# Column maxima of a two-layer graph attention: spread over partitions by a DRAM row instead of by transposes, and scores one step further ahead

## The chip, the core and the metric

The kernel runs on one core of a Trainium2 chip. A core has five engines with a queue each: TensorE (PE in the profile; its weight loads are PEld) multiplies matrices into PSUM, VectorE (DVE) and ScalarE (ACT) work elementwise on SBUF and PSUM, GpSimd (POOL) works on SBUF, and SyncE (SP) issues transfers. ScalarE and GpSimd can issue transfers too. An engine works through its instructions in the order of the program; between engines, semaphores hold an instruction until what it needs is there. The transfers themselves run on 16 DMA engines that the queues share.

The metric is the device time of one execution in microseconds.

## What is computed

There are N = 3327 nodes with D = 512 features. Two layers of attention run first (L = 2, slope 0.01 in the leaky ReLU), with the same dense adjacency mask of zeros and ones:

```
for W in W_stack:                       # two layers
    Wh, Ws = split(x @ W, 2)
    a   = softmax(Wh @ Ws.T, axis=-1) * adj
    x   = leaky_relu(a @ Wh + x)
x = layernorm(x0 + x)                   # x0: the input
xw  = max(sign(x), 0) @ sign(weight).T
out = layernorm(x + relu(adj @ xw))
```

All of the attention is in float32. The softmax needs, for each row of the scores (a query), the row's maximum before the exponential and the sum after it.

## The kernel before

**Tiles.** 3327 rows are NT = 26 tiles of 128, the last with 127 rows. Two tiles make a half chunk (NQ = 13 of them, 256 rows), two half chunks make a chunk (NC = 7, up to 512 rows; the seventh has one half only). Scores are held transposed: keys are on the partitions, queries along the free dimension. A score tile `s` belongs to a half chunk g of queries and a block q of 256 keys: 128 partitions x 2 x 256 float32. The maximum of a query therefore runs over the partitions and over 13 score tiles.

**Stages of a layer.** `project` computes the left and right factors of the scores and the values and stores them to DRAM. `attention` then has one long loop over steps v, with u = v + LOOK. In step v it emits, for the pair (g, q) number v, the aggregation products `values` (L726). For the score pairs, numbered by chunk c, block q and s = 0 or 1, it emits `scores` number u. LOOK = 2 NQ + 4 = 30, so scores run 30 steps ahead; their tiles wait in a ring of SBUFS = 33 SBUF buffers. A layer has 182 score steps and 169 aggregation steps. Hence it begins with steps that have scores alone, goes on with steps that have both, and ends with steps that have aggregation alone.

**Order of the work.** The schedule is written by hand. Each piece of work of a step has a fraction, and the pieces are emitted in order of the fraction (`for _, do in sorted(work, ...)`); every engine keeps that order. A list `after` holds pieces that the next step is to run. For aggregation number v, the step v - 3 emits `shift` (L645, VectorE, fraction 0.0: subtract the query's maximum, the tile `off`) and `exponential` (L648, ScalarE, 0.12). The step v - 2 emits `running` (L656, the sum) and `masked` (L661, the product with the adjacency, then four sums on GpSimd, L699 to L702).

**Scores.** Two score steps make seven products of a Strassen-like scheme (L500). They go to three PSUM banks, X, Y and Z. Between the products to Z, ScalarE copies the bank out (`copied`, L517), and the next product to Z waits for that copy. The order is z1, x2, z6, y5 for s = 0 and z7, y3, z4 for s = 1. VectorE adds up the four quarters and takes the running maximum over the key blocks into `top` (L570). With one half chunk, four plain products and two ScalarE copies (L557) do the same.

**Maxima.** After the last score pair of a chunk (q = 12, s = 1), the three stages of `column_max` are put on `after`:

- `fold` (-0.04): VectorE takes the larger of the two halves of `top` (L594);
- `across` (0.36): TensorE transposes `top` into one PSUM bank (L602, four transposes for a full chunk), VectorE reduces along the free dimension (L605), which leaves each query's maximum in a column of `mx` with queries on the partitions; four multiplications with `ones` (L607) then repeat each column along 128 elements;
- `back` (0.9): TensorE transposes the repeated columns (L612), which puts the maximum of each query on all partitions, and VectorE copies them to `off` (L616), one tile for each half chunk.

For chunk c the last score pair is number 26c + 25. So `across` and `back` stand in step v = 26c - 4, and the first `shift` that reads the new `off` in step 26c - 3. For chunk 0 these steps lie in the part of a layer with scores alone; for chunk 6 they come where the scores have just ended.

**Queues.** SyncE issues all loads of the loop, each some steps ahead: `ws` (two steps), the adjacency (four), `xs` (two) and `gs` (four). GpSimd issues the stores. ScalarE issues no transfer.

Of the kernel before, what the change touches and what calls it, by code (L numbers as in the profile page):

```python
# [9 lines left out]
F32 = mybir.dt.float32  # L10
# [5 lines left out]
ALU = mybir.AluOpType  # L16
# [3 lines left out]
P = 128  # L20
CT = 4
CW = CT * P
HW = CW // 2
# [6 lines left out]
def kernel(  # L30
# [8 lines left out]
    nc = tc.nc  # L39
    N, D = x.shape  # L40
    L = w_stack.shape[0]
# [3 lines left out]
    NC = -(-NT // CT)  # L45
    NQ = NT // 2
# [8 lines left out]
    def halves_of(c):  # L55
        return [g for g in (2 * c, 2 * c + 1) if g < NQ]
# [9 lines left out]
    keep = ctx.enter_context(tc.tile_pool(name="keep", bufs=1))  # L66
# [4 lines left out]
    ps_acc = ctx.enter_context(tc.tile_pool(name="ps_acc", bufs=4, space=PSUM))  # L71
    ps_tr = ctx.enter_context(tc.tile_pool(name="ps_tr", bufs=1, space=PSUM))

    LOOK = 2 * NQ + 4
    SBUFS = LOOK + 3

    def slot(shape, dtype, name):
        return ring.tile(shape, dtype, tag="s", bufs=SBUFS, name=name)
# [2 lines left out]
    make_identity(nc, ident)  # L81
    ident_h = keep.tile([P, P], BF16, name="ident_h")
    nc.vector.tensor_copy(ident_h, ident)
    ones = keep.tile([P, P], F32, name="ones")
    nc.vector.memset(ones, 1.0)
    eps = keep.tile([P, 1], F32, name="eps")
    nc.vector.memset(eps, EPS)
    mv = keep.tile([P, NT, 2], F32, name="mv")
# [17 lines left out]

    xs_d = [tc.dram_tile([NQ, P, 8, 2, P], F32, name=f"xs_d{l}") for l in range(L)]
    ws_d = [tc.dram_tile([NQ, P, 4, HD], F32, name=f"ws_d{l}") for l in range(L)]
    gs_d = [tc.dram_tile([NC, P, 7, 2, HW], F32, name=f"gs_d{l}") for l in range(L)]

    def load_rows(eng, dst, src, r):
# [357 lines left out]
    def attention(l, att):  # L469
# [35 lines left out]
        def scores(c, q, s):  # L505


            mine = halves_of(c)
            if s == 0:
                for i in mine:  # L510
                    sc[i, q] = slot([P, 2, HW], F32, f"s_{l}_{i}_{q}")
            lo, hi = sc[mine[0], q], sc[mine[-1], q]
            c11, c21, c12, c22 = lo[:, 0], lo[:, 1], hi[:, 0], hi[:, 1]

            def copied(name, bank):
                ch[name] = att.tile([P, HW], F32, tag=name, bufs=1, name=f"{name}_{l}_{c}_{q}")
                nc.scalar.copy(ch[name], ch[bank])  # L517

            def z1():
                product(c, q, "Z", A11, B11, True)  # L520
                copied("p1", "Z")

            def x2():
                product(c, q, "X", A12, B21, True)

            def add11():
                nc.vector.tensor_tensor(c11, ch["X"], ch["p1"], ALU.add)

            def z6():
                product(c, q, "Z", S2, T2, False)  # L530
                copied("u2", "Z")

            def y5():
                product(c, q, "Y", S1, T1, True)
                copied("p5", "Y")

            def z7():
                product(c, q, "Z", S3, T3, False)
                copied("u3", "Z")

            def add22():
                nc.vector.tensor_tensor(c22, ch["p5"], ch["u3"], ALU.add)  # L542

            def y3():
                product(c, q, "Y", S4, B22, False)

            def add12():
                nc.vector.tensor_tensor(c12, ch["Y"], ch["u2"], ALU.add)

            def z4():  # L550
                product(c, q, "Z", A22, T4, False)
                nc.scalar.copy(c21, ch["Z"])

            def direct(a, k):
                product(c, q, "D", (A11, A12, A21, A22)[2 * a + k], (B11, B21)[k], k == 0)
                if k:
                    nc.scalar.copy(lo[:, a], ch["D"])  # L557

            def maximum(i):
                t = sc[i, q]  # L560
                if q == NQ - 1 and pad:
                    nc.vector.tensor_scalar(
                        t[:, 1], t[:, 1], there[:, 0:1], there[:, 1:2], ALU.mult, ALU.add
                    )
                if q == 0:
                    top[i] = att.tile([P, 2, HW], F32, tag=f"top{i % 2}", bufs=1,
                                      name=f"top_{l}_{i}")
                    nc.vector.tensor_copy(top[i], t)
                else:
                    nc.vector.tensor_tensor(top[i], top[i], t, ALU.max)  # L570

            if s == 1:

                after.append((-0.05, lambda: maximum(mine[0])))
                if q == NQ - 1:
                    after.extend(column_max(c))
            if len(mine) == 1:
                return [(0.2, lambda: direct(s, 0)), (0.6, lambda: direct(s, 1))]
            if s == 0:
                return [(0.06, z1), (0.31, x2), (0.45, add11), (0.56, z6), (0.81, y5)]  # L580
            return [
                (0.02, z7), (0.2, add22), (0.35, y3), (0.5, add12), (0.68, z4),
                (0.62, lambda: maximum(mine[-1])),
            ]

        def column_max(c):

            n = len(tiles_of(c))
            mx = small.tile([P, CT], F32, tag="mx", name=f"mx_{l}_{c}")
            rep = [top[g][:, 1, ts(a, P)] for g in halves_of(c) for a in range(2)]  # L590

            def fold():
                for g in halves_of(c):
                    nc.vector.tensor_tensor(  # L594
                        top[g][:, 0], top[g][:, 0], top[g][:, 1], ALU.max
                    )

            def across():
                pt = ps_tr.tile([P, CT, P], F32, tag="tr", name=f"ptop_{l}_{c}")
                for i, g in enumerate(halves_of(c)):  # L600
                    for a in range(2):
                        nc.tensor.transpose(  # L602
                            pt[:, 2 * i + a, :], top[g][:, 0, ts(a, P)], ident
                        )
                nc.vector.reduce_max(mx[:, :n], pt[:, :n, :], axis=AX.X)  # L605
                for a in range(n):
                    nc.vector.tensor_scalar(rep[a], ones, mx[:, a : a + 1], None, ALU.mult)  # L607

            def back():
                pb = ps_tr.tile([P, CW], F32, tag="tr", name=f"poff_{l}_{c}")  # L610
                for a in range(n):
                    nc.tensor.transpose(pb[:, ts(a, P)], rep[a], ident)  # L612
                for i, g in enumerate(halves_of(c)):
                    off[g] = att.tile([P, 1, HW], F32, tag=f"off{i}", bufs=1,
                                      name=f"off_{l}_{g}")
                    nc.vector.tensor_copy(off[g][:, 0], pb[:, ts(i, HW)])  # L616

            return [(-0.04, fold), (0.36, across), (0.9, back)]

        def load_adj(g, q):  # L620
            i0, n = half_cols(g)
# [255 lines left out]
        blocks.update(  # L877
            {room[n * len(room) // len(late)]: steps[i] for n, i in enumerate(late)}
        )
        later, after = [], []  # L880
        for v in range(-LOOK - 4, len(steps)):
            u = v + LOOK

            if 0 <= v + WS - 1 < len(steps):
                load_ws(*steps[v + WS - 1])
            if 0 <= v + 4 < len(steps):
                load_adj(*steps[v + 4])
                if blocks.get(v + 4, steps[v + 4]) != steps[v + 4]:
                    load_adj(*blocks[v + 4])
            for lead, load in ((2, load_xs), (4, load_gs)):  # L890
                if 0 <= u + lead < len(ahead):
                    c, q, h = ahead[u + lead]
                    if h == 0 and (lead == 2 or q == 0):
                        load(c, q)
            work, after = after, []
            if 0 <= v + 3 < len(steps):
                s3 = steps[v + 3]
                work += [(0.0, lambda: shift(*s3)), (0.12, lambda: exponential(*s3))]
            if 0 <= v + 2 < len(steps):
                s2 = steps[v + 2]  # L900
                work += [(0.01, lambda: running(*s2)), (0.4, lambda: masked(*s2))]
                of = blocks.get(v + 2)
                if of:
                    work += [
                        (0.6, lambda: halved_sums(*of)), (0.62, lambda: exact(*of)),
                        (0.61, lambda: halved(*of)),
                    ]
                    after.append((0.5, lambda of=of: keep_blocks(*of)))
            if later:
                work += [(0.7, later.pop(0))]  # L910
            if 0 <= u < len(ahead):
                work += scores(*ahead[u])
            if v >= 0:
                work += values(*steps[v])
            if not last:
                work += early.get(v, [])
            for _, do in sorted(work, key=lambda e: e[0]):
                do()
            if v >= 0 and steps[v][1] == NQ - 1:
                later += finish(steps[v][0])  # L920
            if last:
                load_products(v)
# [266 lines left out]
```

## Time and profile before

| What | Value |
|---|---|
| Median of 3 runs | 2652.95 us (2652.05 to 2653.69) |
| The profiled execution, its own time | 2652.55 us |
| Span of the profiled execution | 2650.7 us |
| Mean granted TensorE clock | 0.998 |
| TensorE busy | 2614.6 us, 99% |
| VectorE busy | 2046.3 us, 77% |
| ScalarE busy | 812.1 us, 31% |
| GpSimd busy | 1091.3 us, 41% |
| Moved by DMA | 638.63 MB, 241 GB/s in the mean |

How to read the lines that follow. L726 is line 726 of the kernel. Busy times are in us, the mean of one instruction is in ns. A group has the line, the engine, the operation, what it writes and reads by the program's names, the shape, the count, then busy time and mean, and last the idle time of the engine just before these instructions with what ended it. A line of the timeline begins with the start and the duration in us; a bracket at its end holds the idle time before it and the releaser. A matmul's end is modelled and overlaps the next one, so the cost of one in TensorE's stream is the distance between starts. A line of the windows has the window, its length, each engine's busy time with the number of instructions, the granted clock, the DMA engines' share and GB/s.

### The profile page before, as it was taken

Reading aid. Unit: us, or ns where it says so; the run is one execution under the profiler, and the core shown is the slowest. Engines: PE = TensorE matmul, PEld = TensorE weight load, DVE = VectorE, ACT = ScalarE, POOL = GpSimd, SP = SyncE. Lnnn points to the kernel's source line nnn. Section 1 sums busy time; section 2 is a strip of 40 time slices with the busy share of each in tenths; the row PEclk is TensorE's granted clock in tenths of the full one; section 3 lists DMA queues with packets and bytes.
Section 4 is the critical chain, followed back from the end, with each engine's and each line's share of the span. In section 5 each row is a group of like instructions: output and inputs, shape, how many; then the busy total and the mean of one; then the engine's idle time right before and its main releaser. Section 6 shows DMA issues by size and latency. Waiting matters only on the chain. (4 is left out here: it accounts for less than half of the span.)

```text
span 2650.7 us, 40451 instructions
## 1 busy us (share of the span) xinstructions
PE 2614.6 (99%) x12839; PEld 2271.0 (86%) x12864; DVE 2046.3 (77%) x4211; ACT 812.1 (31%) x2000; POOL 1091.3 (41%) x2029
## 2 busy tenths in 40 slices
PE   9999999999999999999999999999999999999998
PEld 7888888888888888887888888888888888888787
DVE  5554888899888896666754589988899888767976
ACT  3333332333333332221333333333333333222143
POOL 2550343444444444546552044444444444455510
PEclk9999999999999999999999999999999999999999
DMA  5754777777777776776865677777777777677875
GB/s 205 272 193 157 260 239 251 253 266 252 259 244 244 267 248 222 235 245 230 294 219 180 210 231 272 241 257 260 233 270 247 252 255 236 228 260 260 278 245 168
DMA packets 285186, 638.63 MB, mean 241 GB/s; under 512 B 32141, under 2 KB 146671, under 8 KB 283430
## 3 DMA queue, kind: packets, MB, share of 16 engines
q1 hardware_dynamic: 249206, 529.52, 60.4%
q0 software_dynamic: 35760, 106.45, 10.8%
q8 instruction: 105, 1.72, 0.3%
q14 instruction: 115, 0.94, 0.1%
HBM read 528.91 MB, written 106.93 MB: 240 GB/s over the span
## 5 line engine op out<-in xcount | busy, mean ns | idle before, releaser
L500 PE MATMUL pZ<-gs,xs 128*128 128x256 f32 x2496 | 636.2, 379 | 1.7 <-ACT u L517 1.7
L699 POOL TENSOR_TENSOR as<-s 128x128 f32<-128x128 f32 x338 | 163.4, 484 | 1037.0 <-DVE s L661 691.9
L500 PEld LDWEIGHTS pZ<-gs,xs 128*128 128x128 f32 x2496 | 473.3, 190 | 67.8 <-ACT u L517 3.6
L726 PE MATMUL acc<-ws,s 128*128 128x256 f32 x1352 | 402.6, 379 | 0.0
L726 PE MATMUL acc<-wh,s 128*128 128x256 f32 x1352 | 355.9, 379 | 0.0
L726 PE MATMUL acc<-ws,as 128*128 128x256 f32 x1352 | 349.7, 380 | 1.8 <-POOL as L701 1.2
L648 ACT ACTIVATE s<-s 128x512 f32<-128x512 f32 x338 | 213.3, 631 | 377.7 <-DVE s L645 377.1
L500 PE MATMUL pY<-gs,xs 128*128 128x256 f32 x1248 | 320.7, 379 | 2.2 <-ACT p L517 2.2
L726 PEld LDWEIGHTS acc<-ws,as 128*128 128x128 f32 x1352 | 255.2, 190 | 42.3 <-issue 5.8
L726 PEld LDWEIGHTS acc<-wh,s 128*128 128x128 f32 x1352 | 257.3, 190 | 35.2
L726 PEld LDWEIGHTS acc<-ws,s 128*128 128x128 f32 x1352 | 256.2, 190 | 34.4
L570 DVE TENSOR_TENSOR top<-top,s 128x512 f32<-128x512 f32 x312 | 225.4, 735 | 69.0 <-ACT s L557 48.5
L500 PEld LDWEIGHTS pY<-gs,xs 128*128 128x128 f32 x1248 | 236.7, 190 | 36.0 <-ACT p L517 3.8
L645 DVE TENSOR_TENSOR s<-s,off 128x512 f32<-128x512 f32 x338 | 249.2, 737 | 0.1
L661 DVE TENSOR_TENSOR s<-s,adj 128x512 f32<-128x512 f32 x338 | 236.8, 701 | 9.4 <-DMA adj<-in_adjT_dram 1.0
L656 DVE TENSOR_TENSOR total<-total,s 128x512 f32<-128x512 f32 x312 | 231.8, 743 | 0.0
L517 ACT COPY u<-pZ 128x256 f32<-128x256 f32 x312 | 115.8, 371 | 345.5 <-PE pZ L500 344.9
L701 POOL TENSOR_TENSOR as<-s 128x128 f32<-128x128 f32 x338 | 204.7, 606 | 26.5
L726 PE MATMUL acc<-wh,as 128*128 128x256 f32 x676 | 203.0, 382 | 0.0
L700 POOL TENSOR_TENSOR s<-s 128x128 f32<-128x128 f32 x338 | 183.3, 542 | 27.6
L702 POOL TENSOR_TENSOR as<-s,as 128x128 f32<-128x128 f32 x338 | 180.7, 535 | 26.5
L542 DVE TENSOR_TENSOR s<-p,u 128x256 f32<-128x256 f32 x156 | 66.8, 428 | 151.7 <-ACT u L517 151.7
(206 smaller groups left out, 3883.9 us busy)
## 6 DMA issues: line engine op xcount, KB each, us to landing
ws<-ws_d SPq DMA_DIRECT2D x338, 512.0 KB, 3.8
xs<-xs_d SPq DMA_DIRECT2D x182, 512.0 KB, 5.8
adj<-in_adjT_dram SPq DMA_DIRECT2D x324, 256.0 KB, 4.2
xs<-xs_d SPq DMA_DIRECT2D x156, 384.0 KB, 6.5
gs_d<-gsp POOLq DMA_DIRECT2D x88, 256.0 KB, 2.8
gs<-gs_d SPq DMA_DIRECT2D x12, 1792.0 KB, 10.9
adj_d<-ab POOLq DMA_DIRECT2D x169, 112.0 KB, 3.8
ahl<-adj_d SPq DMA_DIRECT2D x78, 224.0 KB, 4.7
```

What stands on the lines that cost most here:

```text
L500: nc.tensor.matmul(ch[bank], xs[c, q, a][:, k], gs[c][:, b, k], start=(start and k == 0), stop=(k == 1), skip_group_check=True,)
L517: nc.scalar.copy(ch[name], ch[bank])
L570: nc.vector.tensor_tensor(top[i], top[i], t, ALU.max)
L645: nc.vector.tensor_tensor(s, s, off[g].to_broadcast([P, 2, HW]), ALU.subtract)
L648: nc.scalar.activation(sc[g, q], sc[g, q], AF.Exp)
L656: nc.vector.tensor_tensor(total[g], total[g], sc[g, q], ALU.add)
L661: nc.vector.tensor_tensor(s, s, adj[g, q], ALU.mult)
L699: nc.gpsimd.tensor_tensor(s3, a11, a21, ALU.subtract)
L700: nc.gpsimd.tensor_tensor(a21, a21, a22, ALU.add)
L701: nc.gpsimd.tensor_tensor(s2, a21, a11, ALU.subtract)
L702: nc.gpsimd.tensor_tensor(s4, a12, s2, ALU.subtract)
L726: nc.tensor.matmul(acc[g][i // 2][:, i % 2], a[i], b[i], start=(q == 0 and i % 2 == 0), stop=(q == NQ - 1), skip_group_check=True,)
```

## The change

The `back` stage no longer uses TensorE and VectorE. `across` ends with a DMA, issued by ScalarE, that stores `mx` to a row of 512 floats in DRAM (`off_d`, one row for each chunk and layer). `back` consists of one DMA for each half chunk, issued by ScalarE too, which reads 256 floats of that row onto each of the 128 partitions of `off`. The four multiplications with `ones`, the second four transposes and the copies out of PSUM are gone, and with them the tile `ones`.

`back` moves one step later than `across` (list `after_next`) and to the fraction 0.15. LOOK becomes 31: for chunk c, `across` now stands in step v = 26c - 5, `back` in 26c - 4, and the first `shift` that reads `off` still in 26c - 3. The ring of score tiles stays at 33 buffers, as SBUFS is now LOOK + 2.

```diff
@@ -71,8 +71,8 @@
     ps_acc = ctx.enter_context(tc.tile_pool(name="ps_acc", bufs=4, space=PSUM))
     ps_tr = ctx.enter_context(tc.tile_pool(name="ps_tr", bufs=1, space=PSUM))
 
-    LOOK = 2 * NQ + 4
-    SBUFS = LOOK + 3
+    LOOK = 2 * NQ + 5
+    SBUFS = LOOK + 2
 
     def slot(shape, dtype, name):
         return ring.tile(shape, dtype, tag="s", bufs=SBUFS, name=name)
@@ -81,8 +81,6 @@
     make_identity(nc, ident)
     ident_h = keep.tile([P, P], BF16, name="ident_h")
     nc.vector.tensor_copy(ident_h, ident)
-    ones = keep.tile([P, P], F32, name="ones")
-    nc.vector.memset(ones, 1.0)
     eps = keep.tile([P, 1], F32, name="eps")
     nc.vector.memset(eps, EPS)
     mv = keep.tile([P, NT, 2], F32, name="mv")
@@ -106,6 +104,7 @@
 
     xs_d = [tc.dram_tile([NQ, P, 8, 2, P], F32, name=f"xs_d{l}") for l in range(L)]
     ws_d = [tc.dram_tile([NQ, P, 4, HD], F32, name=f"ws_d{l}") for l in range(L)]
+    off_d = [tc.dram_tile([NC, CW], F32, name=f"off_d{l}") for l in range(L)]
     gs_d = [tc.dram_tile([NC, P, 7, 2, HW], F32, name=f"gs_d{l}") for l in range(L)]
 
     def load_rows(eng, dst, src, r):
@@ -573,7 +572,8 @@
 
                 after.append((-0.05, lambda: maximum(mine[0])))
                 if q == NQ - 1:
-                    after.extend(column_max(c))
+                    for part, stages in zip((after, after_next), column_max(c)):
+                        part.extend(stages)
             if len(mine) == 1:
                 return [(0.2, lambda: direct(s, 0)), (0.6, lambda: direct(s, 1))]
             if s == 0:
@@ -587,7 +587,6 @@
 
             n = len(tiles_of(c))
             mx = small.tile([P, CT], F32, tag="mx", name=f"mx_{l}_{c}")
-            rep = [top[g][:, 1, ts(a, P)] for g in halves_of(c) for a in range(2)]
 
             def fold():
                 for g in halves_of(c):
@@ -603,19 +602,19 @@
                             pt[:, 2 * i + a, :], top[g][:, 0, ts(a, P)], ident
                         )
                 nc.vector.reduce_max(mx[:, :n], pt[:, :n, :], axis=AX.X)
-                for a in range(n):
-                    nc.vector.tensor_scalar(rep[a], ones, mx[:, a : a + 1], None, ALU.mult)
+                nc.scalar.dma_start(
+                    out=off_d[l][c].rearrange("(a p) -> p a", p=P)[:, :n], in_=mx[:, :n]
+                )
 
             def back():
-                pb = ps_tr.tile([P, CW], F32, tag="tr", name=f"poff_{l}_{c}")
-                for a in range(n):
-                    nc.tensor.transpose(pb[:, ts(a, P)], rep[a], ident)
                 for i, g in enumerate(halves_of(c)):
                     off[g] = att.tile([P, 1, HW], F32, tag=f"off{i}", bufs=1,
                                       name=f"off_{l}_{g}")
-                    nc.vector.tensor_copy(off[g][:, 0], pb[:, ts(i, HW)])
-
-            return [(-0.04, fold), (0.36, across), (0.9, back)]
+                    nc.scalar.dma_start(
+                        out=off[g][:, 0], in_=off_d[l][c][ts(i, HW)].partition_broadcast(P)
+                    )
+
+            return [(-0.04, fold), (0.36, across)], [(0.15, back)]
 
         def load_adj(g, q):
             i0, n = half_cols(g)
@@ -877,7 +876,7 @@
         blocks.update(
             {room[n * len(room) // len(late)]: steps[i] for n, i in enumerate(late)}
         )
-        later, after = [], []
+        later, after, after_next = [], [], []
         for v in range(-LOOK - 4, len(steps)):
             u = v + LOOK
 
@@ -892,7 +891,7 @@
                     c, q, h = ahead[u + lead]
                     if h == 0 and (lead == 2 or q == 0):
                         load(c, q)
-            work, after = after, []
+            work, after, after_next = after, after_next, []
             if 0 <= v + 3 < len(steps):
                 s3 = steps[v + 3]
                 work += [(0.0, lambda: shift(*s3)), (0.12, lambda: exponential(*s3))]
```

## The prediction

> **What bounds the kernel now.** I read the page's first two parts first, to find the engine that sets the end; then the groups of instructions, for the lines that the edit touches; then the timeline around one of the fourteen places where they run; last the windows and DMA landings there.
>
> ```profile
> PE 2614.6 (99%) x12839; PEld 2271.0 (86%) x12864; DVE 2046.3 (77%) x4211; ACT 812.1 (31%) x2000; POOL 1091.3 (41%) x2029
> PE   9999999999999999999999999999999999999998
> ```
>
> TensorE has no free slice, and its gaps over 0.15 us add up to 22.5 us, of which the first 5.6 us wait for x. So a microsecond taken out of its stream is a microsecond of time, and one that any other engine saves is worth nothing by itself.
>
> ```profile
> L607 DVE TENSOR_SCALAR top<-ones,mx 128x128 f32<-128x128 f32 x52 | 11.5, 282 | 0.5
> L616 DVE COPY off<-poff 128x256 f32<-128x256 f32 x26 | 9.8, 415 | 3.1 <-PE poff L612 3.1
> L605 DVE TENSOR_REDUCE mx<-ptop 128x4 f32<-128x512 f32 (+1 forms) x14 | 9.1, 648 | 6.4 <-PE ptop L602 6.4
> L602 PE MATMUL ptop<-ident,top 128*128 128x128 f32 x52 | 8.3, 279 | 2.7 <-DVE top L594 2.6
> L612 PE MATMUL poff<-ident,top 128*128 128x128 f32 x52 | 8.0, 274 | 0.6 <-DVE wTs L123 0.6
> ```
>
> Of these the edit deletes L607, L612 and L616 and keeps L602 and L605. The 274 ns of L612 overlap the next matmul; the cost in the stream is read from start to start, here in layer 0's first chunk, where scores run without aggregation:
>
> ```profile
> 276.68 0.68 PE L602 MATMUL ptop<-ident,top 128*128 128x128 f32 x4 [0.57 <-DVE top L594]
> 277.20 1.03 PE L500 MATMUL pZ<-gs,xs 128*128 128x256 f32 x4
> 277.40 0.69 DVE L605 TENSOR_REDUCE mx<-ptop 128x4 f32<-128x512 f32 x1 [0.53 <-PE ptop L602]
> 278.06 1.03 PE L500 MATMUL pY<-gs,xs 128*128 128x256 f32 x4
> 278.31 0.37 ACT L517 COPY u<-pZ 128x256 f32<-128x256 f32 x1 [2.66 <-PE pZ L500]
> 278.93 0.60 PE L612 MATMUL poff<-ident,top 128*128 128x128 f32 x4
> 279.36 1.03 PE L500 MATMUL pZ<-gs,xs 128*128 128x256 f32 x4
> 280.24 0.68 DVE L645 TENSOR_TENSOR s<-s,off 128x512 f32<-128x512 f32 x1
> 280.95 0.63 ACT L648 ACTIVATE s<-s 128x512 f32<-128x512 f32 x1
> ```
>
> Four transposes hold TensorE from 278.93 to 279.36. The same lines show the tight spot: the copy u of one pZ product must end before the next pZ product may overwrite the bank. It ended at 278.68, some 0.25 us before the poff slot began; in this stretch ScalarE's copies have that little to spare.
>
> **What the Trainium skill says.** "DMA: Bandwidth & Descriptors", Anatomy of one DMA: about 2.0 us of a DMA is fixed, mostly the receipt of the last write, and waits are held on the issuing sequencer. The trace agrees on the size: the shortest small landings are 1.9 and 2.0 us. The same page, Rules for kernel authors: a DMA that reads what another wrote waits for its completion, and a strided last dimension becomes one descriptor per element. No transfer of the kernel before is of that kind. Same page, Queues, rings and completion order: a DMA engine takes turns between queues packet by packet, so a new queue doesn't stand behind SyncE's whole backlog; POOL's own queue below is the case to compare. "Perfetto Trace Analysis", DMA Instruction — HWDGE: the issuing sequencer is held while descriptors are generated. SyncE's issues are mostly 0.32 to 0.47 us here; ScalarE issues none yet.
>
> **What goes.** 12 full chunks x 0.43 us of L612 = 5.2, and two half chunks x 0.21 (2444.22 to 2444.43 in layer 1) = 0.4, plus L612's wait in layer 0's last chunk, 0.6: 6.2 us of TensorE. 52 x 0.28 of L607 and 26 x 0.41 of L616 are about 21 us less busy VectorE, worth nothing while TensorE doesn't wait for it. The memset of ones is one instruction before the first matmul's data land: nothing.
>
> **What comes.** Per chunk one write of the maxima and two reads (one in the half chunks) that spread 1 KB rows to 128 partitions, all on ScalarE's queue. The write has 512 elements of 4 bytes, 32 for each of 16 engines. I bound its landing W, from issue: below by the shortest landing, about 2.0, plus its issue and packets, 2.4 us; above, if each 4-byte packet takes its turn behind one 4 KB packet of SyncE at 0.16 us, 2.0 + 32 x 0.16 = 7.1 us. I take 3.6, a third of the way up, because the queues aren't always full. The read R moves 128 KB in 1 KB packets, like POOL's stores of adj_d:
>
> ```profile
> L684 POOL DMA_DIRECT2D adj_d<-ab x169: 557/557/569, 292.8 to 2242.7; - x169
> DMA to landing us min/median/max: 2.0/3.8/7.5
> ```
>
> 2.0 to 7.5, median 3.8; a ScalarE issue near SyncE's 0.4 instead of 0.56 makes it 3.6, and a read doesn't end on DRAM: I take 3.1, range 2.2 to 5. What matters is X = W + R: 6.7 us, from 4.6 to about 11. DMA is far from idle there (last two numbers: share, GB/s):
>
> ```profile
> 277.00:283.00 6.00, 6.00 (x32) 5.33 (x32) 4.92 (x14) 2.12 (x5) 0.00 (x0) 1.00 0.81 266
> 1509.00:1515.00 6.00, 5.42 (x30) 4.45 (x29) 5.17 (x14) 1.75 (x5) 0.00 (x0) 1.00 0.92 300
> 428.00:434.00 6.00, 6.00 (x31) 5.28 (x30) 5.86 (x15) 1.59 (x5) 2.51 (x5) 1.00 0.56 188
> 2443.00:2449.00 6.00, 6.00 (x31) 5.25 (x31) 5.72 (x10) 1.19 (x2) 3.87 (x7) 1.00 0.94 334
> ```
>
> Whether X is hidden depends on the stage. The extra step of lookahead is worth one step's time: 6.05 us where scores and aggregation alternate, 3.03 where one of them runs alone (a pair of score steps repeats every 6.05: the pZ at 279.36 returns at 285.41).
>
> *First chunk of a layer (2 places), score steps only.* The write is ready at 278.1. After it come the write's landing, the read's landing, L645 0.7, L648 0.65, the next u copy 0.4 and hand-overs 0.15: 280.0 + X. That copy must end before the pZ that falls at 285.0 once poff is gone. So TensorE waits X - 5.0 us: 1.7 each, 3.4 together (0 to 12). L648 stands in ScalarE's order ahead of that copy, hence a late off tile stops TensorE. The write's issue also holds the first u copy until about 278.5, which costs 0.3 each: 0.6.
>
> *Middle chunks (10 places).* From the reduction to the first L645 that needs off there are 1.46 steps of TensorE's order plus a copy and a maximum, less the transposes and reduction: 8 to 8.8 us. A further 2.7 us pass before a copy that TensorE needs stands behind L648. X of 6.7 is hidden; the cover ends near X = 11. If it were gone (each round trip 1 us too long) it would cost 10 us. ScalarE, held for the write, has the final c21 copy behind it, not due for 3 us. Cost 0.
>
> *Last chunk (2 places), aggregation only.* mx ends at 2443.54, L645 follows at 2445.09 and gains one step of 3.03: 4.6 us. X + 0.3 makes it 2.4 late. Next late are L656 and L661 on VectorE, POOL's four sums, then aggregation two steps on, with about 3.2 us in hand. Cost X - 7.5 when positive: 0 now.
>
> *One step further ahead.* Scores and aggregation have the same matmuls in both orders; no work added. SBUF stays at 33 score buffers, so the spare one goes, but a new score tile is first written after products that TensorE executes after the freeing matmuls: no wait. Weight loads, wT tiles and the aggregated rows in the same ring fit, at 33 of 33 in the worst step, and SyncE's next ws load waits for that same step anyway. ScalarE's DMAs share the descriptor generator with SyncE; xs and ws are issued steps early, so some 0.5 us is hidden.
>
> **Sum.** 6.2 removed, 3.4 + 0.6 given back: 2.2 us less. The profiled execution took 2652.55 us, of which 2650.7 are span: 2650.35. The median of the runs, 2652.95, lies 0.4 above it; so I forecast 2650.8.
>
> **Rivals.** *The round trip is short* (X up to 5.2): almost nothing is given back, 2646.9. For it: landings down to 1.9 us. Against: DMA shares of 0.8 to 0.9 in the first chunks. *The round trip is the new wait*: the 4-byte packets alternate with SyncE's, W = 7.1, R = 3.6, X = 10.7. First chunks 2 x 5.7, issue 0.6, last chunks 2 x 3.2 = 18.4, less 6.2: 2665, slower. Breakeven is near X = 7.7 and the loss passes 0.2% at X = 9. The 7.5 us maximum of POOL's stores speaks for it, their median against it. A read of one row by 128 descriptors could be slower than any transfer here; at X = 13 each middle chunk would also lose some 2 us, past 2685. *ScalarE itself*: issues of a microsecond instead of 0.4 would delay every later copy; ten middle chunks have slack, so about 2 us more, 2653.
>
> **How the numbers follow.** A gain can hardly pass 0.3%, and 0.2% (5.3 us) is about what a measurement of this kernel can tell from no change. Within it: X between 5.2 and 9, chance 0.43, own range 2648 to 2658, the long issue included. Faster by more: X under 5.2, 0.27. Slower by more: X over 9, 0.30, of which a tenth lies past 2664. The range is 2646 to 2664.
>
> **What would show it.** Right: poff gone, TensorE's stream some 5.6 us shorter; a gap before pZ of 1 to 2 us in each layer's first chunk, released by ScalarE's u copy; L645 there waiting for the DMA into off; no new TensorE gap in middle chunks; write landings of 3 to 4 us. Wrong: landings over 5 us each, L645 waiting in middle chunks too, or gaps at the places where aggregation runs alone.

## The result, and the profile after

| | Before | After |
|---|---|---|
| Median of 4 runs each | 2652.57 us (2652.05 to 2653.69) | 2733.14 us (2732.16 to 2737.6) |
| The profiled execution: own time, span | 2652.55, 2650.7 us | 2737.6, 2735.7 us |
| Mean granted TensorE clock | 0.998 | 0.988 |
| TensorE busy, and the sum of the gaps between its instructions | 2614.6 + 24.6 us | 2639.4 + 85.0 us |

The kernel became slower by 80.6 us, a ratio of 1.0307 (95% interval 1.0295 to 1.0319). The forecast was 2650.8, the range ended at 2664. TensorE's order is shorter, as the deleted transposes are gone. Yet it has 60.4 us more gaps, and its busy time grew by 24.8 us. Together these are 85.2 us, and the spans differ by 85.0.

The first two parts of the page after, TensorE's busy time and its slices with the granted clock below:

```profile
PE 2639.4 (96%) x12812; PEld 2276.2 (83%) x12812; DVE 2028.0 (74%) x4132; ACT 806.6 (29%) x2000; POOL 1095.2 (40%) x2029
PE   9999899999999999999999899999999999999898
PEclk9999899999999999999999999999999999999999
```

Where a row of nines stood there are 8s, and the first of them falls in a slice with a lower clock. The busy time grew by more than it seems, as the transposes to `poff` (8.0 us busy before) are deleted. The groups of the edit after; every line number is one lower than before, so L604 and L644 answer to L605 and L645. The last line is L645 in the kernel before:

```profile
L604 DVE TENSOR_REDUCE mx<-ptop 128x4 f32<-128x512 f32 (+1 forms) x14 | 9.1, 647 | 2.6 <-PE ptop L601 2.4
L644 DVE TENSOR_TENSOR s<-s,off 128x512 f32<-128x512 f32 x338 | 249.4, 738 | 71.0 <-DMA off<-off_d 71.0
L645 DVE TENSOR_TENSOR s<-s,off 128x512 f32<-128x512 f32 x338 | 249.2, 737 | 0.1
```

The three deleted groups are gone. The subtraction takes as long as before, but VectorE now waits 71.0 us for `off` ahead of it. The waits of after show what reaches TensorE (total, count and longest; the last line is of the kernel before):

```profile
DVE s L644 <- DMA off<-off_d: 71.0, 13, 14.3
PE pZ L499 <- ACT u L516: 24.7, 14, 3.4
PE pZ L499 <- ACT p L516: 19.4, 7, 6.8
PE pZ L500 <- ACT u L517: 1.7, 2, 1.0
```

There are thirteen waits for `off`, the longest of 14.3 us, and two lines of the scores' copies. In the kernel before, pZ waited 1.7 us for u and not at all for p. The transfers themselves, on ScalarE's queue:

```profile
L613 ACTq DMA_DIRECT2D off<-off_d x26: 325/386/1430, 288.3 to 2523.1; - x26
L605 ACTq DMA_DIRECT2D off_d<-mx x14: 377/377/394, 278.3 to 2513.8; - x14
DMA to landing us min/median/max: 5.8/7.9/10.5
```

The last line is over both kinds. Taken apart in the trace, the write lands after 7.3 to 10.5 us, median 9.4, and a read after 5.8 to 8.6, median 7.5. From the write's issue to the landing of the chunk's first read, the round trip X is 14.3 to 17.4 us, median 16.5. Layer 0's first chunk, the place that the prediction shows too:

```profile
278.31 0.39 ACTq L605 DMA_DIRECT2D off_d<-mx  x1
288.28 1.48 ACTq L613 DMA_DIRECT2D off<-off_d  x2
289.94 0.37 ACT L551 COPY s<-pZ 128x256 f32<-128x256 f32 x1 [9.11 <-issue]
290.63 2.08 PE L499 MATMUL pZ<-gs,xs 128*128 128x256 f32 x4 [6.83 <-ACT p L516]
295.74 0.69 DVE L644 TENSOR_TENSOR s<-s,off 128x512 f32<-128x512 f32 x1 [4.97 <-DMA off<-off_d]
297.41 2.07 PE L499 MATMUL pZ<-gs,xs 128*128 128x256 f32 x4 [2.99 <-ACT u L516]
```

Two stops follow from one round trip. The reads wait on ScalarE for the write to land, so the copy L551 stands behind them for 9.11 us, and TensorE for 6.83. Then the exponential waits for `off`, the copy u behind it, and TensorE for another 2.99. The four matmuls at 290.63 show a second price: 2.08 us for a group that took 1.03. In the record of the granted clock, 17.07 us from 285.99 on are at half speed, and near most of the other long gaps there are stretches of 3.41 or 6.83 us, 58 us in all ahead of the kernel's tail; before had one such stretch, of 3.41 us.

The windows (columns as in the prediction: each engine's busy time, then clock, DMA share, GB/s) show a third thing. The first line is the kernel before, the other two are after:

```profile
284.00:292.00 8.00, 8.00 (x39) 7.03 (x38) 7.82 (x16) 3.12 (x9) 3.97 (x7) 1.00 0.92 316
```

```profile
284.00:292.00 8.00, 1.36 (x3) 1.18 (x4) 0.43 (x1) 0.65 (x2) 0.00 (x0) 0.62 0.62 87
443.00:449.00 6.00, 6.00 (x29) 5.29 (x28) 2.40 (x6) 0.33 (x2) 2.51 (x5) 1.00 0.39 42
```

While the write is out, the DMA engines move next to nothing for anyone. That is so in a middle chunk too, where TensorE's order still hides it: 42 GB/s from 443 to 449. The kernel before moved 229 GB/s in that window, and 165 in the one that lies as far behind its own maxima (431.7 to 437.7).

### The profile page after: what moved, and what is told of

It reads as the page before. It is cut to its first block, busy times and chain, and to the rows that moved or that the text cites. A ratio compares the mean times of both kernels' runs of the same rounds, so it can differ in the third digit from the quotient of the medians.

```text
span 2735.7 us, 40384 instructions
## 1 busy us (share of the span) xinstructions
PE 2639.4 (96%) x12812; PEld 2276.2 (83%) x12812; DVE 2028.0 (74%) x4132; ACT 806.6 (29%) x2000; POOL 1095.2 (40%) x2029
## 3 DMA queue, kind: packets, MB, share of 16 engines
q0 software_dynamic: 35760, 106.45, 10.5%
## 5 line engine op out<-in xcount | busy, mean ns | idle before, releaser
L499 PE MATMUL pZ<-gs,xs 128*128 128x256 f32 x2496 | 644.9, 383 | 44.2 <-ACT u L516 24.7
L644 DVE TENSOR_TENSOR s<-s,off 128x512 f32<-128x512 f32 x338 | 249.4, 738 | 71.0 <-DMA off<-off_d 71.0
L660 DVE TENSOR_TENSOR s<-s,adj 128x512 f32<-128x512 f32 x338 | 238.8, 706 | 10.5 <-POOL s L699 1.4
## 6 DMA issues: line engine op xcount, KB each, us to landing
gs<-gs_d SPq DMA_DIRECT2D x12, 1792.0 KB, 11.1
```

The lines of the kernel that those rows point to most:

```text
L499: nc.tensor.matmul(ch[bank], xs[c, q, a][:, k], gs[c][:, b, k], start=(start and k == 0), stop=(k == 1), skip_group_check=True,)
L644: nc.vector.tensor_tensor(s, s, off[g].to_broadcast([P, 2, HW]), ALU.subtract)
L660: nc.vector.tensor_tensor(s, s, adj[g, q], ALU.mult)
```

## The experiments

Theories at the start: the round trip is the new wait; or the later stage with its longer lookahead costs the time; or the extra traffic does. All medians stand against runs of the kernel before on the same chip, 2652.7 to 2653.2 us. Line numbers differ a little between the kernels.

### The edit taken apart

**The later stage alone.** The kernel before with LOOK 31, 33 buffers and its old `back` (transposes and all) in the next step:

```diff
+    LOOK = 2 * NQ + 5
+    SBUFS = LOOK + 2
...
+            return [(-0.04, fold), (0.36, across)], [(0.15, back)]
```

> The kernel before with the changed lookahead alone: 31 steps, 33 buffers, and the old second stage (transposes of the repeated maxima and copies out of PSUM) moved to the later step at 0.15. Theory (the DRAM round trip is the whole loss): no change, 2650 to 2655 us, no new TensorE gaps. Rival (the lookahead with a full ring of score tiles is what stalls): most of the 80 us is here, 2700 us or more, with gaps where score tiles are written.

2657.23 us, ratio 1.0018 (1.0011 to 1.0024): 4.4 us of the loss. There is a new gap of 2.02 us before a pZ, with 3.41 us of half clock behind it, and there are waits of up to 1.1 us for `fold`.

**No spreading at all**, from after: neither the write nor the reads. A constant stands for the maxima, and the exponential is taken of a hundredth of its argument; this holds for every run below that leaves the maxima out.

```diff
-                nc.scalar.dma_start(out=off_d[l][c]...
...
+                    off[g] = flat
```

> The changed kernel with neither the write nor the reads: a constant stands for the maxima, and the exponential is taken of a hundredth of its argument so that it stays finite, so the spreading is left out altogether. Theory: the removal alone is worth the 6.2 us of TensorE that were predicted, 2645 to 2648 us. Rival (the later step or the full ring costs something too): above 2655 us.

2650.16 us, ratio 0.9988 (0.9979 to 0.9996): 7.1 us below the run above. So everything beyond that, 83.0 us, comes from the two kinds of transfer. The gap of e1's kind is still there, without any DMA to wait for:

```profile
292.98 0.63 ACT L642 ACTIVATE s<-s 128x512 f32<-128x512 f32 x1 [3.21 <-DVE s L639]
293.52 0.35 ACT L518 COPY u<-pZ 128x256 f32<-128x256 f32 x1
293.93 1.13 PE L501 MATMUL pZ<-gs,xs 128*128 128x256 f32 x4 [2.03 <-ACT u L518]
```

At LOOK 31 the exponential stands directly ahead of a copy u that TensorE needs, and VectorE gets to the subtraction late, since its mask work and the running maximum come first.

**The write alone**: the run above with after's write, and nothing that waits for it.

```diff
+                nc.scalar.dma_start(
+                    out=off_d[l][c].rearrange("(a p) -> p a", p=P)[:, :n], in_=mx[:, :n]
+                )
```

> The kernel without any spreading (constant maxima, exponential of a hundredth) plus the element-wise write, which nothing waits for. Theory (512 writes of 4 bytes freeze the DMA engines for all queues): most of the 62 us that separate the kernel with reads of x from the one without spreading is here, 2690 to 2712 us, with SyncE's transfers late. Rival (the write only hurts whoever waits for it; the reads of x did the damage): within 3 us of the kernel without spreading, 2647 to 2653 us.

2667.4 us, ratio 1.0052 (1.0035 to 1.0069). Fourteen transfers of at most 2 KB that nobody reads cost 17.2 us, and still land after 7.6 to 10.1 us. That is more than the rival allowed and far less than the theory asked for. TensorE's new gaps wait for SyncE's loads: 4.23 us for `xs`, 2.43 and 3.49 for `ws`.

**The reads don't wait for the write**: they take a row of x, the write stays.

```diff
-in_=off_d[l][c][ts(i, HW)].partition_broadcast(P)
+in_=x[c, ts(i, HW)].partition_broadcast(P)
```

> The changed kernel in which the reads take a row of x instead of the row of maxima, so they no longer wait for the write, which is still issued (the exponential is taken of a hundredth of its argument; the maxima are left out). Theory: ScalarE's queue is not held, the read alone (7.2 us from issue to landing) stands against the slack; about 2 us in each first chunk and little elsewhere, less the 6.2 us of TensorE, plus what the element-wise write does to SyncE's transfers: 2650 to 2662 us. Rival (the read is the larger half of the loss): above 2680 us.

2712.31 us, ratio 1.0227 (1.0209 to 1.0244). This is the outcome that was named as the rival. Reads that are issued directly behind the write land after 8.7 to 14.9 us, median 11.1, and VectorE waits 88.2 us for them. So that ScalarE and the reads wait for the write explains only the last 20.8 us.

**The reads alone**: the same, without the write.

```diff
-                nc.scalar.dma_start(out=off_d[l][c]...
```

> No write, and the reads take one row of x onto all partitions without waiting for anything (exponential of a hundredth). Theory (the reads are harmless once the write is gone): landing of 4 to 5 us as with the row write, and 2650 to 2656 us. Rival (the reads of one row by 128 descriptors are slow by themselves): landing of 6 us or more and 2665 us or more.

2651.73 us, ratio 0.9997 (0.9988 to 1.0005), 1.6 above no spreading. A read lands after 3.4 to 6.2 us, median 4.6. Reading one row onto 128 partitions is harmless by itself. So the write alone costs 17.2 us and the reads alone 1.6, but the two side by side, without any wait of one for the other, cost 62.2: most of the 83.0 us is the price of reads held up beside the write.

**The write as four rows**: one more transpose turns `mx` into 4 rows of 512 bytes, which are written instead.

```diff
+            def row():
+                pr = ps_tr.tile([CT, P], F32, tag="tr", name=f"prow_{l}_{c}")
+                nc.tensor.transpose(pr[:n], mx[:, :n], ident)
...
+                nc.scalar.dma_start(
+                    out=off_d[l][c].rearrange("(a p) -> a p", p=P)[:n], in_=mr[:n]
+                )
```

> The changed kernel with the write alone redone: one transpose turns the four columns of maxima into four rows, and the DMA stores 4 rows of 512 bytes instead of 512 elements of 4 bytes. Theory (the element-wise write is slow by itself, 9.5 us from issue to landing, and holds up SyncE's transfers too): the write lands in 2.5 to 4 us, the reads come 5 to 6 us earlier, and the time falls to 2665 to 2680 us, since a round trip of 10 to 11 us still stands out in the first and last chunks. Rival (every transfer on ScalarE's queue stands behind SyncE's backlog): the write still takes 6 us or more and the time stays above 2700 us.

2661.95 us, ratio 1.0036 (1.0022 to 1.0051): 71.2 of the 80.6 us are gone with the form of the write alone, somewhat more than was expected. In the first chunk the reads, which wait for the write, issue 1.57 us after it; the three reads whose landing the trace holds land after 4.1 to 5.5 us. The group of the subtraction:

```profile
L650 DVE TENSOR_TENSOR s<-s,off 128x512 f32<-128x512 f32 x338 | 246.3, 729 | 13.8 <-DMA off<-off_d 13.8
```

13.8 us of waiting are left of 71.0.

### What in the write it is

Both go on the kernel with the write alone. **Each element 512 bytes from the next**: the same 512 pieces of 4 bytes.

```diff
+    off_d = [tc.dram_tile([NC, CW, P], F32, name=f"off_d{l}") for l in range(L)]
...
+                    out=off_d[l][c].rearrange("(a p) e -> p a e", p=P)[:, :n, 0:1],
```

> As the last, but each of the 512 elements of 4 bytes goes to a place 512 bytes from the next, instead of 512 neighbours within 2 KB. If it is the neighbours (engines that take turns at the same few lines of DRAM) that freeze the engines: a landing of 4 us or less and 2648 to 2658 us. If it is the number of tiny writes: as the dense write, 2690 us or more.

2650.4 us, ratio 0.9991 (0.9982 to 0.9999), landing 1.6 to 4.7 us. **128 pieces of 16 bytes** in the same 2 KB:

```diff
+    off_d = [tc.dram_tile([NC, P, CT], F32, name=f"off_d{l}") for l in range(L)]
...
+                nc.scalar.dma_start(out=off_d[l][c][:, :n], in_=mx[:, :n])
```

> As the write of neighbours, but 128 descriptors of 16 bytes (each partition's four maxima together) instead of 512 of 4 bytes, into the same 2 KB. If the cost goes with the number of descriptors: a quarter of the dense write's, 2660 to 2668 us, and a landing of 4 to 5 us. If any write smaller than a line does it: near the dense write. If it is below 2655 us, the cost is not linear in the number.

2649.9 us, ratio 0.9988 (0.9981 to 0.9995), landing 1.4 to 4.8 us. Neither costs anything. The DMA view from 278 to 295 us in 40 slices (GB/s), with SyncE's weights and the write below it (KB each, us to landing), for the plain write alone:

```profile
GB/s 260 210 366 92 50 24 58 0 0 0 0 0 10 19 39 29 29 0 29 0 10 19 19 29 0 19 19 106 299 320 333 395 465 414 393 376 405 439 414 349
ws<-ws_d SPq DMA_DIRECT2D x3, 512.0 KB, 10.3
off_d<-mx ACTq DMA_DIRECT2D x1, 2.0 KB, 9.3
```

and for the spaced one:

```profile
GB/s 169 229 282 354 309 72 29 15 77 154 299 299 308 96 0 87 173 166 145 296 335 349 381 347 395 429 453 349 386 410 424 426 378 398 402 429 398 361 383 243
ws<-ws_d SPq DMA_DIRECT2D x3, 512.0 KB, 6.4
off_d<-mx ACTq DMA_DIRECT2D x1, 2.0 KB, 2.6
```

Both show 528 packets on ScalarE's queue in this window. In the first chunk of after, the plain write's packets have all begun 1.8 us after its issue, and then every queue stands nearly still for some 8 us. So it is neither the number of small packets nor their turns with SyncE's. Nor is it the small stretch of DRAM alone, as 16-byte pieces fill the same 2 KB. What is left is 4-byte pieces that lie side by side. The time doesn't grow with their number: the half chunks write 256 of them, and in after these land as late, after 9.4 and 9.2 us. Distances between 4 and 512 bytes were not tried, and why neighbours collide was not seen: the trace shows the standstill, not its inside.

### The lookahead

All three are without spreading. **34 buffers instead of 33** at LOOK 31, **LOOK 30 with 33**, and **LOOK 32 with 34**:

```diff
-    SBUFS = LOOK + 2
+    SBUFS = LOOK + 3
```

> No spreading (constant maxima in one column, exponential of a hundredth), 31 steps of lookahead, but 34 buffers in the ring, so one is to spare again. If the full ring is what makes the lookahead alone 4.4 us slower: 2645 to 2647 us. If it is the other order of the work (which of an odd and an even step meets a chunk's end): as with 33 buffers, 2649 to 2651 us.

```diff
-    LOOK = 2 * NQ + 5
-    SBUFS = LOOK + 2
+    LOOK = 2 * NQ + 4
+    SBUFS = LOOK + 3
```

> No spreading at 30 steps of lookahead with 33 buffers, as the kernel before but without the second transposes, the repeated columns and the copies. Prediction's step: 6.2 us less than the kernel before, 2645.5 to 2647.5 us; together with the version at 31 steps it shows what the lookahead costs without any spreading, 3 to 5 us.

```diff
-    LOOK = 2 * NQ + 5
+    LOOK = 2 * NQ + 6
```

> No spreading (constant maxima in one column, exponential of a hundredth), 32 steps of lookahead and 34 buffers. If the odd lookahead is what costs (a chunk's end falls on the heavier of two alternating steps in the other layer): near the version at 30 steps, 2641 to 2645 us. If each step of lookahead costs: 2653 us or more. If 31 and 32 are alike: 2648 to 2651 us.

2649.9 (0.9986, 0.998 to 0.9993), 2642.53 (0.9958, 0.9942 to 0.9975) and 2646.02 us (0.9972, 0.9962 to 0.9982). The full ring costs nothing. Thirty-one steps cost 7.6 us against thirty, with no transfer of the maxima in play (7.4 on one chip, against the run with 34 buffers); thirty-two give about half of it back, 1 us less than was expected if the odd step were all. The gap at 293.9 us is absent at 30 and at 32. TensorE's waits for a copy u, at 31, 30 and 32 steps:

```profile
PE pZ L501 <- ACT u L518: 5.2, 6, 2.0
PE pZ L501 <- ACT u L518: 1.3, 2, 0.7
PE pZ L501 <- ACT u L518: 1.3, 2, 0.7
```

So about half of the price goes with 31 being odd; that an odd step changes which copy stands behind an exponential fits this, but was read from the one place above. What the remaining 3.5 us at 32 are stays open. At LOOK 30, deleting the spreading is worth 10.7 us, more than the 6.2 us that were expected.

### Can a row in DRAM pay at all?

**Pieces of 8 bytes**, from after: each half chunk's maxima interleaved in pairs, the subtraction reads `off` at a stride of two floats.

```diff
+                    out=off_d[l][c].rearrange("i p a -> p i a")[:, : n // 2],
...
+            turned = off[g].rearrange("m o (p a) -> m o a p", a=2)
```

> The changed kernel, complete, with the maxima stored as 8-byte pieces (one for each partition and half chunk) in the order partition, tile; the reads stay 1 KB rows, and the subtraction reads the row in that order. If only writes of 4 bytes into neighbouring places freeze the engines: write landing 3 to 4 us, reads 4 to 5, and 2653 to 2662 us. If 8 bytes still do: landing of 6 us or more and 2680 us or more. A slower subtraction from the strided order would show in its mean of 738 ns.

**Pieces of 16 bytes**: one read of 2 KB for each chunk, a stride of four floats.

```diff
+                    out=off_d[l][c][: P * n].rearrange("(p a) -> p a", a=n), in_=mx[:, :n]
...
+                    off[g] = both[:, :, : P * n].rearrange("m o (p a) -> m o a p", a=n)[
+                        :, :, 2 * i : 2 * i + 2
+                    ]
```

> As the last with one piece of 16 bytes for each partition and one read of a 2 KB row for the whole chunk, which has to wait until the last subtraction of the chunk before. Theory: the write is as harmless as it was alone (3.4 us), the read of 256 KB takes 5 to 6 us and starts later, so 2654 to 2665 us, with waits for the read at middle chunks too.

2669.44 us (1.0059, 1.0043 to 1.0076) and 2702.81 us (1.0182, 1.0165 to 1.0199). With 8 bytes the write lands after 4.8 us in the median, and the kernel is 63.7 us faster than after. With 16 bytes it lands after 2.8, and yet the kernel is slower. Both missed what was expected, the first by 7 us. The subtraction's group with 8 bytes, and then with 16:

```profile
L647 DVE TENSOR_TENSOR s<-s,off 128x512 f32<-128x512 f32 x338 | 248.7, 736 | 38.8 <-DMA off<-off_d 38.8
```

```profile
L647 DVE TENSOR_TENSOR s<-s,off 128x512 f32<-128x512 f32 x338 | 376.8, 1115 | 29.1 <-DMA off<-off_d 29.1
```

The wait shrank further, but the mean of the 338 subtractions rose from 736 to 1115 ns: 128 us more VectorE, which has no such room where scores run (7.82 of 8 us busy in the first window shown above). TensorE's waits for copies u rose from 13.1 to 21.7 us, and those of `across` for `fold` from 4.1 to 10.7. The trace has its own control: the half chunks hold two columns, so their 26 subtractions read at a stride of two and took 769 ns on average; the other 312 took 1144. The Trainium skill ("SBUF — State Buffer", Door 1: The DMA port swizzle) says that accesses run at full speed while at least two of them fall into one 16-byte line. A stride of two floats keeps that, one of four does not, and both runs agree. The same note gives four float32 as the stride that is free; that doesn't hold here.

**Four rows, LOOK 32**, the two reads one and two steps after the write, to give the round trip more cover; for space the ring of GpSimd's sums `as` has two tiles instead of three.

```diff
+    LOOK = 2 * NQ + 6
...
+                [(0.15, lambda: back(0))], [(0.15, lambda: back(1))],
...
+                t = att.tile([P, 3, P], F32, tag="as", bufs=2, name=f"as_{l}_{g}_{q}")
```

> Complete: four rows of 512 bytes written, 32 steps of lookahead, 34 buffers, the first half chunk's read one step after the maxima and the second's two steps after; to make room the four rows lie in a used-up part of top, and the ring of GpSimd's sums has 2 buffers instead of 3. Theory (only the uncovered part of the round trip is left, and an even lookahead is free): 2643 to 2649 us, faster than the kernel before. Rival (reads onto all partitions cost by contention, or the lookahead costs): 2655 us or more. The smaller ring of sums could add waits of aggregation for GpSimd; they would show as such.

2735.6 us (1.0309, 1.0292 to 1.0327), a miss. VectorE waits for `off` only 0.7 us, once; but GpSimd's first sum now waits 671.1 us for aggregation to free a tile. TensorE's gaps are 87.0 us. The smaller ring hid what was asked. **The same with three tiles**, the space taken from elsewhere (a sum and two late tiles overwrite their sources):

```diff
+                t = att.tile([P, 3, P], F32, tag="as", bufs=3, name=f"as_{l}_{g}_{q}")
...
+                out_["u3"] = out_["p1"]
```

> Complete: 32 steps of lookahead and 34 buffers, four rows of 512 bytes written, the halves read one and two steps after the maxima, sums with 3 buffers again; the room comes from tiles that are written a second time in place (u3 over p1; the transposed signs and the product's half-precision copy over the signs). Theory (the uncovered part of the round trip was all that was left, an even lookahead is nearly free): 2645 to 2651 us, faster than the kernel before. Rival (the reads cost by contention): 2655 us or more.

2654.83 us (1.0009, 1.0002 to 1.0015), the best of the kernels with a row in DRAM. Its waits for `off` are 2.4 us, and TensorE's gaps 27.5. It was to be faster than before and is not: the same LOOK without spreading stands at 2646.02, so the row, its transpose, its waits and the tiles that overwrite their sources still cost 8.8 us, more than the 7.0 us by which that run is below the kernel before. What those tiles cost alone was not run, nor was a row at 30 steps. **And with after's write in it**:

```diff
-            [(-0.04, fold), (0.36, across), (0.6, row)],
+            [(-0.04, fold), (0.36, across)],
```

> As the last, but with the 512 elements of 4 bytes of the changed kernel. If only latency counted, two more steps hide most of its 17 us round trip: 2650 to 2660 us. If the frozen DMA engines count, the write alone keeps its 17 us and the reads and ScalarE's wait for the write add to it: 2670 us or more.

2708.65 us (1.0207, 1.0193 to 1.0221), 53.8 above the row. VectorE waits 43.4 us for `off`, pZ up to 5.7 us for a copy p, and aggregation 4.22 and 3.65 us for `ws`. More lookahead covers a late tile, but neither a standstill of all queues nor ScalarE's hold for the write. Reads that another engine issues were not tried.

## Why the prediction was wrong

"The round trip is the new wait" was the rival that came true, and beyond its own numbers: it went up to an X of 13 us and "past 2685", with 0.03 of chance past 2664. In the order of the prediction's steps:

*What goes.* Right in kind: the time of L612's transposes did leave TensorE. 6.2 us were forecast; the runs show 7.1 at LOOK 31 and 10.7 at LOOK 30. There TensorE's busy time fell by 5.9 us, near the forecast, and its gaps by 3.8, of which the forecast had 0.6.

*The landing of the write, W.* This is the step that failed. It was bounded at 2.4 to 7.1 us and taken as 3.6; it is 9.4 in the median, above the upper bound. The bound let each 4-byte packet take its turn behind one 4 KB packet of SyncE. The spaced write has the same packets and the same turns and lands after 3.5, which is nearly the number chosen; that it is so near is partly luck, as the number was a guess between the bounds. The model held for a write that this kernel doesn't make. That the price lies in pieces being neighbours was in no view of before, since it has no such write. The Trainium skill's rule on a strided last dimension ("DMA: Bandwidth & Descriptors", Rules for kernel authors: one descriptor for each element) was read as a count of packets. The 2.0 us of fixed cost under the lower bound are stated on that page for transfers that GpSimd issues; on ScalarE's queue the write in 16-byte pieces landed after 1.4 us at the shortest.

*The read, R.* Taken as 3.1, range to 5. Alone it is 4.6, inside that range; after the write it is 7.5. In the first chunk the reads are issued shortly before SyncE's held loads resume. In the run that reads x directly behind the write, R is 11.1. So 1.5 us of the miss are the read's own, and the rest comes with the write.

*First, middle and last chunks.* The places were right, and with the measured X the forms give sums of the right size, all somewhat too high. X of 17.4 and 16.5 makes X - 5.0 12.4 and 11.5 us for the first chunks; TensorE's gaps in the 40 us after the write are 10.0 and 8.9. For the last chunks X - 7.5 gives 9.0 and 9.7; there are 6.8 and 8.7, of which the kernel before had 0.8 and 3.3. For the middle ones X lies 3 to 6 us above the cover of 11, and their gaps are 0.9 to 4.5 each. But the way there is only partly the forecast's, as the next step shows.

*ScalarE, held for the write.* Wrong. For the middle chunks the forecast allowed 3 us until the copy behind the held reads is due, and for the first chunks it counted only the write's issue, 0.3 each. The hold in layer 0 is 9.11 us. It makes TensorE's longest gap (6.83), and the exponential behind the late `off`, which the forecast named, makes the smaller one (2.99).

*A new queue doesn't stand behind SyncE's backlog.* The skill's same page, Queues, rings and completion order, says that queues take turns by packet. The spaced write agrees: in the window of 278 to 295 us it landed after 2.6 us, and SyncE's `ws` after 6.4. The reverse was not asked: what the new queue does to SyncE's. In the same window `ws` lands after 10.3 us with the write alone, where before had 5.2, and that write costs 17.2 us without anyone waiting for it.

*One step further ahead: no work, no wait.* It costs 4.4 us (7.6 without the spreading: 2650.16 less 2642.53), which were put at nothing. The full ring is harmless, as said. But the odd step puts an exponential directly ahead of a copy u, the very order which the first-chunk part describes, and it was not applied here.

*What wasn't in the sum.* Gaps as long as these go with a lower clock. The Trainium skill ("TensorE: Matmul & The Clock Gate", Why this matters for your kernels) warns of idle gaps over about 3 us. In this trace stretches of 3.41 us at 0.5 come with gaps from 2.0 us up, though not with all of them, so 3 us is no safe limit here. 24.8 us of busy time came on top of 60.4 us of gaps. An estimate from the clock's record: 54.6 us more at half speed than before are worth at most 27.3 us.

The 80.6 us taken apart, by differences of medians: the later stage +4.4; the spreading's work gone, -7.1; the write by itself +17.2; and the reads and what waits, directly on ScalarE or through them, +65.7 (after less the write alone). They add up to 80.2; the rest lies between the runs of the kernel before on different chips. The last is what reads and waiting cost beside a write of this form; with the write as rows, 71.2 of the 82.9 us go.

A write that lands in time would not have made the forecast come true. With rows, where X is 6.8 us in the first chunk as the forecast had it, the kernel takes 2661.95: inside the range, but 11 us above 2650.8 and slower than before. The extra step is 4.4 to 7.6 of these; the rest was not taken apart.

## What to carry over

Before a small transfer is put on a path to hide latency, look at what its pieces are in DRAM: 512 neighbouring pieces of 4 bytes brought all queues nearly to a stop for 8 us, and the same bytes as four rows, spaced, or in pieces of 16 bytes did not. A bound on a new transfer must include what it does to the transfers of others. And when a lookahead is changed by one in a schedule with a period of two, check again which instruction stands ahead of which on each queue.

## What the runs showed of the hardware

- A write of 512 x 4 bytes into 2 KB of DRAM lands after 9.1 us in the median when nobody waits for it; 3.5 us with the pieces 512 bytes apart, 3.4 as 128 x 16 bytes, 4.8 as 256 x 8 bytes (in a kernel that waits for it). With the plain one, all DMA engines together moved 18 GB/s for 6 us (283 to 289 us), with 16-byte pieces 265. Half as many 4-byte pieces in 1 KB land as late: 9.5 and 8.3 us in the run with the write alone.
- A float32 subtraction on VectorE, 128 x 512, with one operand at a stride of four floats took 1144 ns on average, against 738 without a stride (in after); at two floats 736.
- TensorE's clock went to half for 3.41 us after a gap of only 2.0 us (at 1111.71, and in the run with the later stage alone at 293.83); not after every such gap (in after, none follows that of 2.08 us at 2236.53 or that of 2.93 us at 2571.25).
